# Attention over listed neighbours and a two-of-eight expert layer: gathered-row buffers placed in stage one, second-layer weights loaded from the last values on

## The chip, the cores and the metric

The kernel runs on one core of a Trainium2 chip. The metric is the device time of one execution in microseconds; the median of several runs is compared. One further execution is recorded by the hardware profiler, and all the times inside the kernel come from that one.

## What is computed

There are N = 4096 nodes with 512 features. The reference normalizes them, attends over the neighbours of each node (adjacency plus the node itself) with 8 heads of 64, adds the result to the input, normalizes again and sends each node through the two best of 8 expert networks:

```python
adj = jnp.maximum(adjacency_matrix, eye)
scores = jnp.einsum('hqk,hmk->hqm', q, k) * kd ** (-0.5)
scores = scores + IDENTITY_BIAS * eye - MASK_VAL * (1.0 - adj)
att = jax.nn.softmax(scores, axis=-1)
x = x + jnp.einsum('hqm,hmk,hko->qo', att, v, Wo)
# then, on the normalized x: logits, top 2 of 8 experts, softmax of the two,
h = gelu(jnp.einsum('nd,edh->neh', xf, W1) + b1)
y = jnp.einsum('neh,ehf->nef', h, W2) + b2          # weighted sum of the chosen two
```

The adjacency is sparse and denser for low-numbered nodes. All data are float32.

## The kernel before

The work has three stages, and the nodes are taken in 32 tiles of 128.

**Stage one (lines 186 to 492)** makes keys, values and queries and lists the neighbours. It is a loop of 65 steps, with 8 steps for each block of four tiles. In steps 0 to 3 of a block `project_kv` (L425) makes one tile of keys and values and SP, the engine that issues most transfers, writes it to `kv_d` in HBM (L436); in steps 4 to 7 `project_q` (L438) makes a quarter of the block's queries, and after step 7 SP writes them to `qT_d` (L486). So the last keys and values are made in step 59 and the last queries in step 63. Between these, the transposed adjacency comes in, one 2 MB tile at a time, into three buffers of a pool `adjT` (L258); VectorE (DVE) reduces each to flags (`neighbours`, L262; the last in step 52), and small matrix products, POOL (`begun`, L319) and DVE turn the flags into two lists of row numbers, `key_of` and `mask_of`.

**Stage two (L656 to L982)** is the attention. For each tile the kernel holds a number of chunks of 128 neighbours (28 for the first tile, 8 for the last; 363 in all) and one item for the tile's own nodes: 395 items. Their steps are:

- `fetch` (L714): POOL issues two indirect transfers (L725), one that gathers 128 rows of keys and values from `kv_d` and one that gathers their rows of the adjacency as masks. For the own item SP loads both (L720, L721). There are ten buffers of each in the pool `kv`, and items are fetched nine ahead (`AHEAD`).
- `turn` (L735): TensorE (PE) transposes the keys and ScalarE (ACT) copies them.
- `scores` (L750): PE multiplies, and ACT takes the exponential.
- `masked` (L771): DVE multiplies by the mask.
- `values` (L777): PE adds to the tile's output `po`, and DVE adds to the running sum `acc`.

When a tile is through, its remaining work is spread over the following items in pieces (`piece`, L802): sum, reciprocal, output projection `py`, and the sum with x into a row buffer (L850), which SP writes to `out` (L851). Tiles are joined into groups (seven of 4, then 2, 1 and 1; `GROUPS`, L665). The jobs of a group (`route`, L858) normalize its rows, compute the logits, rank the experts and give each row two places in a table `xs_d`; POOL then scatters the rows there (`route_4`, L591). The row buffers of all groups share one tag with two buffers (L842), and the first write into one is the copy of the row numbers (L845). The first-layer weights `w1` come in during stage two (L947).

After the last item, `finish_routing` (L603) counts the rows of each expert, writes a table of blocks, and has SP write blank rows behind each expert's rows (L650, eight of them) and into a spare block (L644). The spare block's write has to wait for all the scatters, the other eight don't. The second-layer weights `w2`, 8 loads of 1 MB, are issued by ACT after stage two in the text (L988).

**Stage three (L1113 to L1202)** takes 71 blocks of 128 rows: SP loads a block's rows from `xs_d` (L1131), PE multiplies by the two layers, and POOL scatters and adds the result to `out` (L1181).

What sets the order: stage one and the items of stage two are written out by hand (a manual schedule), outside of which a scheduler merges the instructions. Each engine takes its instructions strictly in order, and waits on semaphores. A tile that is placed where an earlier tile lay waits until everything that used the earlier one has ended, and a transfer issued by SP also waits until the one issued eight before it has landed.

Of the kernel before, what the change touches and what calls it, by code (L numbers as in the profile page):

```python
# [10 lines left out]
F32 = mybir.dt.float32  # L11
BF16 = mybir.dt.bfloat16
I32 = mybir.dt.int32
# [6 lines left out]
P = 128  # L20
# [12 lines left out]
def kernel(  # L33
# [31 lines left out]
    nc = tc.nc  # L65
    N, D = x.shape
    H, KD = Wo.shape[0], Wo.shape[1]
    E, _, HID = W1.shape
    DC = D // P
    HC = HID // P  # L70
    NT = N // P
    TB = 512
    NTB = N // TB
    TPB = TB // P
    NP = H * KD // P
    KV = 2 * H * KD
# [5 lines left out]
    W = D + 4  # L82
# [62 lines left out]
    first = const.tile([P, NB], F32, name="first")  # L145
    table = const.tile([1, 2 * NB + E], I32, name="table")
    redo = const.tile([1, 1], I32, name="redo")

    def mean_var(pool, mv, xin, name):

# [27 lines left out]
        nc.scalar.copy(dst, pt)  # L178


    C = N // P
    G = 4
    NX = C + 3
    CHUNK = 14

    with tc.tile_pool(name="adjT", bufs=3) as ap, tc.tile_pool(
        name="wqkv", bufs=1
    ) as wp, tc.tile_pool(name="p1", bufs=3) as work, tc.tile_pool(
        name="p1b", bufs=2
    ) as block, tc.tile_pool(name="lists", bufs=2) as lp, tc.tile_pool(  # L190
        name="ps1t", bufs=2, space=PSUM
# [6 lines left out]

        xts = {}

        def load_x(i):
            xts[i] = work.tile([P, D], F32, tag="xt", bufs=6, name=f"xt_{i}")
            nc.sync.dma_start(out=xts[i], in_=x[ts(i, P), :])

        for i in range(TPB):
            load_x(i)
        for n, src, queue in (("k", Wks, nc.scalar), ("v", Wvs, nc.scalar), ("q", Wqs, nc.sync)):
            for c in range(DC):
                queue.dma_start(out=w[n][:, c], in_=src[ts(c, P), :])
# [243 lines left out]
            tokens_2(t)  # L453
            tokens_3(t)
        for t in range(TPB):
            load_x(TPB + t)
        list_constants()


        load_at = {13 * i // 8: i for i in range(NT)}  # L460
        lists_from = {13 * (g * G + G - 1) // 8 + 3: g for g in range(NTB)}
        for u in range(8 * NTB + 1):
            b, s = divmod(u, 8)
            if u in load_at:
                load_adj(load_at[u])
            due = []
            for k in range(8):
                if u - k in lists_from:
                    due += lists_at(lists_from[u - k], k)
            nxt = (b + 1) * TPB  # L470
            if b < NTB:
                if b + 1 < NTB:
                    if s < 4:
                        tokens_1(nxt + s)
                    else:
                        tokens_2(nxt + s - 4)
                        if b + 2 < NTB:
                            load_x(nxt + TPB + s - 4)
                if s < 4:
                    project_kv(b, s)  # L480
                else:
                    if s == 4:
                        qT = block.tile([P, NP, TB], F32, tag="qT", name=f"qT_{b}")
                    project_q(b, s - 4, qT)
                    if s == 7:
                        nc.sync.dma_start(out=qT_d[:, :, ts(b, TB)], in_=qT)  # L486
                if b + 1 < NTB and s >= 4:
                    tokens_3(nxt + s - 4)
            if u - 2 in load_at:
                neighbours(load_at[u - 2])  # L490
            for f in due:
                f()

# [109 lines left out]
    def finish_routing(pool, psum, blank):  # L603
# [41 lines left out]
        for e in range(E):  # L645
# [5 lines left out]
            for t in scatters:  # L651
# [4 lines left out]
    w1_cm = tc.tile_pool(name="w1", bufs=1)  # L656
    w1p = w1_cm.__enter__()
    w1 = w1p.tile([P, E, DC, HID], F32, name="w1")
    blank = w1p.tile([P, W], F32, name="blank")
    nc.vector.memset(blank, 0.0)  # L660
    nc.gpsimd.iota(blank[:, D : D + 1].bitcast(I32), pattern=[[0, 1]], base=N,
                   channel_multiplier=1)
    nc.sync.dma_start(out=out[N : N + P, :], in_=blank[:, :D])
    AHEAD = 9
    GROUPS = [4] * (NT // 4 - 1) + [2, 1, 1]  # L665
    with tc.tile_pool(name="kv", bufs=AHEAD + 1) as kvp, tc.tile_pool(
        name="p2", bufs=4
    ) as work, tc.tile_pool(name="p2a", bufs=2) as two, tc.tile_pool(
        name="p2o", bufs=1
    ) as single, tc.tile_pool(name="p3", bufs=2) as small, tc.tile_pool(  # L670
        name="ps_s", bufs=3, space=PSUM
    ) as ps_s, tc.tile_pool(name="ps_o", bufs=1, space=PSUM) as ps_o, tc.tile_pool(
        name="ps_k", bufs=1, space=PSUM
    ) as ps_k, tc.tile_pool(name="ps_e", bufs=2, space=PSUM) as ps_e:
        order = tc.manual_schedule()
        order.__enter__()
        ones32 = single.tile([P, Q4], F32, name="ones32")
# [11 lines left out]
        for p in range(NP):  # L689
            u, j = divmod(p, 2)  # L690
            for r in range(2):
# [2 lines left out]
                    spread[:, p, r * KD : (r + 1) * KD],  # L694
                    ident[:, row : row + 1].to_broadcast([P, KD]),
                )
        q_in, x_in, kv, mask, kT, es, po, acc = {}, {}, {}, {}, {}, {}, {}, {}
        items = [(i, c) for i in range(NT) for c in range(-1, listed[i])]
        group_of, groups = {}, []
        for m in GROUPS:  # L700
            i0 = sum(GROUPS[: len(groups)])
# [1 line left out]
            for i in range(i0, i0 + m):  # L703
                group_of[i] = len(groups) - 1

        def load_q(i):
            q_in[i] = two.tile([P, NP, P], F32, tag="q", name=f"q_{i}")
            nc.sync.dma_start(out=q_in[i], in_=qT_d[:, :, ts(i, P)])

        def load_x(i):  # L710
            x_in[i] = two.tile([P, D], F32, tag="xt", name=f"xr_{i}")
            nc.sync.dma_start(out=x_in[i], in_=x[ts(i, P), :])

        def fetch(n):  # L714

            i, c = items[n]
            kv[n] = kvp.tile([P, KV], F32, tag="kv", name=f"kv_{i}_{c}")
            mask[n] = kvp.tile([P, P], F32, tag="mask", name=f"mask_{i}_{c}")
            if c < 0:
                nc.sync.dma_start(out=kv[n], in_=kv_d[ts(i, P), :])  # L720
                nc.sync.dma_start(out=mask[n], in_=adjT[i, ts(i, P), :])  # L721
                return
            s = slice(at[i] + c, at[i] + c + 1)
            for to, src, of in ((kv[n], kv_d, key_of), (mask[n], adjT_rows, mask_of)):
                nc.gpsimd.indirect_dma_start(  # L725
                    out=to, out_offset=None, in_=src,
                    in_offset=bass.IndirectOffsetOnAxis(ap=of[:, s], axis=0),
                )

            if waiting and n % 3 == 0:  # L730
                waiting.pop(0)[1]()

        waiting = []

        def turn(n):  # L735
            kT[n] = work.tile([P, NP, P], F32, tag="kT", bufs=3, name=f"kT_{n}")
# [65 lines left out]
        def piece(i, k):  # L802
# [14 lines left out]
            if k == 2:  # L817
                rinv[i] = single.tile([P, P], F32, tag="rinv", name=f"rinv_{i}")
                nc.vector.reciprocal(rinv[i], sums[i])
                test = single.tile([P, P], F32, tag="test", name=f"test_{i}")  # L820
                nc.scalar.activation(test, sums.pop(i), AF.Copy, accum_out=fine[:, i, 0:1])
                load_x(i)
            if k == 3:
                rb[i] = ps_e.tile([P, NP, P], F32, tag="e", name=f"rb_{i}")
                for p in range(NP):
# [12 lines left out]
            if k == 6:  # L838
                if j == 0:
                    while waiting and waiting[0][0] < g - 1:  # L840
                        waiting.pop(0)[1](True)
                    row[g] = small.tile([P, m, W], F32, tag="rows", name=f"rows_{g}")  # L842
                    lg[g] = small.tile([P, m, E], F32, tag="l", name=f"l_{g}")
                    mv[g] = small.tile([P, m, 4], F32, tag="mv", name=f"mv_{g}")
                    nc.vector.tensor_copy(  # L845
                        row[g][:, :, D].bitcast(I32), ids[:, i0 : i0 + m]
                    )

                y = row[g][:, j, :D] if m > 1 else x_in[i]
                nc.vector.tensor_add(y, x_in[i], py.pop(i))  # L850
                nc.sync.dma_start(out=out[ts(i, P), :], in_=y)  # L851
                mean_var(small, mv[g][:, j], y, f"b{i}")
                if j == m - 1:
                    jobs.extend(route(g))
                if m > 1:
                    x_in.pop(i)
# [70 lines left out]
                if then:  # L927
                    first_of_step.append(then)

        load_q(0)  # L930
        for n in range(AHEAD):
            fetch(n)
        for n in range(3):
            turn(n)
        for n in range(2):
# [3 lines left out]
        for n, (i, c) in enumerate(items):  # L939
            begin()  # L940
            if n + AHEAD < len(items):
                fetch(n + AHEAD)
            if c == 2 and i + 1 < NT:
                load_q(i + 1)
            if n >= 56 and n % 7 == 0 and loads:
                e, d = loads.pop(0)
                nc.sync.dma_start(out=w1[:, e, d], in_=W1[e, ts(d, P), :])  # L947
            if c < 0 and i:
                osb[i - 1] = single.tile([P, NP, P], F32, tag="o", bufs=2, name=f"o_{i - 1}")
                nc.scalar.copy(osb[i - 1], po.pop(i - 1))  # L950
            if n + 3 < len(items):
                turn(n + 3)
            if n + 2 < len(items):
                scores(n + 2)
            values(n)
            later(n)
            if n + 2 < len(items):
                masked(n + 2)
            if c == listed[i] - 1:
                left.append((n, i))  # L960
        order.__exit__(None, None, None)
        osb[NT - 1] = single.tile([P, NP, P], F32, tag="o", bufs=2, name=f"o_{NT - 1}")
        nc.scalar.copy(osb[NT - 1], po.pop(NT - 1))
        n = len(items)
        while n <= len(items) + LAST or jobs or first_of_step:
            begin()
# [14 lines left out]
        nc.tensor.matmul(pf[:1], least, ones32[:, :1], start=True, stop=True)  # L981
        nc.vector.tensor_copy(redo, pf[:1])  # L982

    w2_cm = tc.tile_pool(name="w2", bufs=1)
    w2p = w2_cm.__enter__()
    w2 = w2p.tile([P, E, HC, D], F32, name="w2")
    for e in range(E):
        nc.scalar.dma_start(out=w2[:, e], in_=W2[e].rearrange("(c p) f -> p c f", p=P))  # L988
    with tc.tile_pool(name="end", bufs=1) as pool, tc.tile_pool(
        name="ps_end", bufs=1, space=PSUM  # L990
    ) as psum:
# [254 lines left out]
```

## Time and profile before

| | us |
|---|---|
| median of three runs | 2305.06 |
| lowest and highest run | 2304.19, 2316.68 |
| profiled execution, its span | 2313.0 |
| PE, DVE, ACT, POOL busy | 2114.2, 1534.8, 966.5, 1235.4 |
| stage one, first gather of stage two, first row load of stage three | 0 to 409.3, 415.21, 1745.06 |
| gathers on POOL, 363 of each kind: keys and values, masks | 467.3, 444.5 |

The busy times are sums over three stages that have different limits, so the joins between the stages can't be seen in them. A matrix product's end is modelled in the trace, so a busy PE is not necessarily a PE at its peak. In the lines below, a row of the timeline has its start, its duration, the engine, the line of the kernel, the operation, what it writes and reads, how many such instructions are merged in the row, and in brackets the idle time of that engine ahead of it with what ended it. SPq, ACTq and POOLq are the engines' own queues; a transfer's row on SPq is its issue alone and not the transfer. In the page's groups, the first number after the bar is the busy time in all, the second the mean of one in ns, and after the second bar stand the idle time ahead of them and its releaser.

### The profile page before, as it was taken

To read this page: it belongs to the slowest core of one execution; us is meant where nothing else is said; L and a number is where in the kernel's file an instruction comes from. 1 tells how busy PE (TensorE), PEld (TensorE's weight loads), DVE (VectorE), ACT (ScalarE), POOL (GpSimd) and SP (SyncE) were. 2 spreads that over 40 slices of the span, in tenths; PEclk is the share of its full clock that TensorE was granted. 3 is DMA by queue.
4 is the path that set the end of the run, shared out by engine and by line. 5 is a ranking of instruction groups with operands and counts; after the bars stand their busy time and mean duration, and the time that the engine had idled before them with its cause. 6 is when DMAs were issued, how large, how long until landed. Compare 5 with 4: busy or idle time off the path is not lost. (4 is left out here: it accounts for less than half of the span.)

```text
span 2313.0 us, 51031 instructions
## 1 busy us (share of the span) xinstructions
PE 2114.2 (91%) x20304; PEld 1419.3 (61%) x20304; DVE 1534.8 (66%) x2300; ACT 966.5 (42%) x1834; POOL 1235.4 (53%) x943
## 2 busy tenths in 40 slices
PE   7789999789999989989999999999837999999998
PEld 3344444577777777777777777777623444444444
DVE  4889983588888878878878879788752232323232
ACT  2122222455556556556556565556411222222221
POOL 1434331678887787787787878778511121221212
PEclk9899999899999999999999999999958999999999
DMA  7767881677777777767677776767565655565554
GB/s 295 289 240 290 312 309 64 196 217 215 227 223 235 238 223 240 233 221 248 211 232 237 234 236 213 229 210 233 171 214 143 135 133 137 135 143 131 136 138 91
DMA packets 176722, 477.36 MB, mean 206 GB/s; under 512 B 23089, under 2 KB 43569, under 8 KB 172386
## 3 DMA queue, kind: packets, MB, share of 16 engines
q0 software_dynamic: 79232, 249.68, 36.9%
q1 hardware_dynamic: 91874, 213.87, 28.3%
q10 hardware_dynamic: 5376, 10.49, 1.4%
q8 instruction: 165, 2.70, 0.5%
q14 instruction: 75, 0.61, 0.1%
HBM read 402.23 MB, written 71.72 MB: 205 GB/s over the span
## 5 line engine op out<-in xcount | busy, mean ns | idle before, releaser
L775 DVE TENSOR_TENSOR e<-e,mask 128x1024 f32<-128x1024 f32 x363 | 443.8, 1223 | 163.7 <-ACT e L768 161.3
L725 POOL DMA_INDIRECT kv<-kv_d,key_of x363 | 467.3, 1287 | 129.1 <-issue 48.8
L725 POOL DMA_INDIRECT mask<-in_adjT_dram,mask_of x363 | 444.5, 1225 | 111.6 <-issue 80.8
L793 DVE TENSOR_TENSOR acc<-acc,e 128x1024 f32<-128x1024 f32 x363 | 442.6, 1219 | 0.0
L768 ACT ACTIVATE e<-s 128x512 f32<-128x512 f32 x726 | 394.5, 596 | 105.3 <-PE s L758 102.3
L758 PE MATMUL s<-q,kT 64*128 64x128 f32 x5808 | 420.4, 285 | 0.3 <-ACT acc L768 0.3
L787 PE MATMUL po<-e,kv 128*64 128x128 f32 x5808 | 408.1, 284 | 2.8 <-DVE e L775 2.8
L745 ACT COPY kT<-pk 128x512 f32<-128x512 f32 x395 | 231.6, 586 | 347.4 <-PE pk L742 343.7
L758 PEld LDWEIGHTS s<-q,kT 64*128 64x128 f32 x5808 | 371.6, 194 | 0.6 <-ACT acc L768 0.6
L1181 POOL DMA_INDIRECT out_dram<-y,r x71 | 110.8, 1560 | 467.5 <-ACT y L1180 298.4
L787 PEld LDWEIGHTS po<-e,kv 128*64 128x64 f32 x5808 | 318.9, 140 | 48.2 <-DVE e L775 3.2
L324 POOL TENSOR_SCALAR started<-slots,base 128x1152 bf16<-128x1152 f32 (+11 forms) x32 | 126.0, 3941 | 251.2 <-DVE longer L295 156.2
L1145 PE MATMUL ph<-w,xT 128*128 x568 | 258.7, 598 | 1.0 <-ACT xT L178 1.0
L1174 PE MATMUL py<-w,hT 128*128 x568 | 255.6, 593 | 0.9 <-DVE hT L1159 0.9
L742 PE MATMUL pk<-ident,kv 64*128 64x64 f32 x2904 | 171.4, 238 | 76.0 <-DMA kv<-kv_d,key_of 62.0
L742 PEld LDWEIGHTS pk<-ident,kv 64*128 64x128 f32 x2904 | 123.1, 141 | 155.4 <-issue 98.8
L1179 DVE TENSOR_TENSOR y<-py,bb 128x512 f32<-128x512 f32 x71 | 49.1, 691 | 225.6 <-PE py L1174 209.7
L1145 PEld LDWEIGHTS ph<-w,xT 128*128 128x128 f32 x568 | 103.5, 193 | 104.6 <-issue 103.0
L1174 PEld LDWEIGHTS py<-w,hT 128*128 128x128 f32 x568 | 102.7, 191 | 103.9 <-issue 102.7
L267 DVE TENSOR_REDUCE flags<-adjT 128x32 f32<-128x4096 f32 x32 | 140.7, 4402 | 21.6 <-DMA adjT<-in_adjT_dram 21.6
L1150 DVE TENSOR_TENSOR h<-ph,bb 128x512 f32<-128x512 f32 x71 | 49.1, 691 | 141.5 <-PE ph L1145 141.5
L1180 ACT ACTIVATE y<-y,gate 128x512 f32<-128x512 f32 x71 | 51.2, 721 | 213.1 <-DVE y L1179 213.1
(576 smaller groups left out, 2251.0 us busy)
## 6 DMA issues: line engine op xcount, KB each, us to landing
adjT<-in_adjT_dram SPq DMA_DIRECT2D x32, 2048.0 KB
bb<-in_L_ffn_b_dram SPq DMA_DIRECT2D x142, 256.0 KB
r<-xs_d SPq DMA_DIRECT2D x71, 258.0 KB
kv_d<-kv SPq DMA_DIRECT2D x32, 512.0 KB
xt<-in_x_dram SPq DMA_DIRECT2D x32, 256.0 KB
qT_d<-qT SPq DMA_DIRECT2D x8, 1024.0 KB
q<-qT_d SPq DMA_DIRECT2D x32, 256.0 KB
xr<-in_x_dram SPq DMA_DIRECT2D x32, 256.0 KB
```

The costliest lines, as they stand in the source:

```text
L267: nc.vector.tensor_reduce(flags[g][:, j, :], adj_in.pop(i), axis=AX.X, op=ALU.max)
L324: nc.gpsimd.tensor_scalar(started[i], slots[:, :n], base[g][:, j : j + 1], None, op0=ALU.is_ge)
L725: nc.gpsimd.indirect_dma_start(out=to, out_offset=None, in_=src, in_offset=bass.IndirectOffsetOnAxis(ap=of[:, s], axis=0),)
L742: nc.tensor.transpose(pk[:, r, ts(p, KD)], kv[n][half, ts(p, P)], ident[half, half])
L745: nc.scalar.copy(kT[n].rearrange("k p (r j) -> k r p j", r=2), pk[:, :, : NP * KD].rearrange("k r (p j) -> k r p j", p=NP),)
L758: nc.tensor.matmul(s[r][:, p, :], k[rows, p, :], q_in[i][rows, p, :], start=True, stop=True,)
L768: nc.scalar.activation(e[:, r * NP : (r + 1) * NP], s[r], AF.Exp)
L775: nc.vector.tensor_mul(e, e, m.unsqueeze(1).to_broadcast([P, 2 * NP, P]))
L787: nc.tensor.matmul(po[i][r * KD : (r + 1) * KD, p, :], v[:, ts(h, KD)], e[:, r * NP + p, :], start=(c < 0 and p == 0), stop=(c == listed[i ...
L793: nc.vector.tensor_add(acc[i], acc[i], e)
L1145: nc.tensor.matmul(ph, xTs[b][:, c, :], w1[:, bass.ds(es[b], 1), c, :], start=(c == 0), stop=(c == DC - 1),)
L1174: nc.tensor.matmul(py, hTs[b][:, c, :], w2[:, bass.ds(es[b], 1), c, :], start=(c == 0), stop=(c == HC - 1),)
```

## The change

1. The pool `adjT` is opened on the right-hand side of the on-chip memory, and closed in stage one as soon as the last adjacency tile has been reduced (step 52). The pools for gathered rows (`kv`) and queries (`q`) are opened in its place there; the first query tile and the first own item are loaded then, and items 1 to 8 are fetched in step 60. Before, all of them were issued at the start of stage two.
2. The blank tile is made among the constants, and its write to `out` is issued at the start of stage one instead of between the stages.
3. A tile's x rows are loaded at its third item instead of after its last.
4. Row buffers have a tag for each group size: groups of four share two buffers, the group of two has one, and the groups of one have two.
5. After the last item the pools `p2`, `q` and `kv` are closed, and `w2` takes their place. SP issues its eight loads, inside the manual schedule, ahead of the last tile's remaining pieces; before, ACT issued them.

```diff
+    blank = const.tile([P, W], F32, name="blank")
+    nc.vector.memset(blank, 0.0)
+    nc.gpsimd.iota(blank[:, D : D + 1].bitcast(I32), pattern=[[0, 1]], base=N,
+                   channel_multiplier=1)
...
-    with tc.tile_pool(name="adjT", bufs=3) as ap, tc.tile_pool(
+    ap_cm = tc.tile_pool(name="adjT", bufs=3, side="right")
+    ap = ap_cm.__enter__()
...
         list_constants()
+        nc.sync.dma_start(out=out[N : N + P, :], in_=blank[:, :D])
...
                 neighbours(load_at[u - 2])
+                if load_at[u - 2] == NT - 1:
+                    ap_cm.__exit__(None, None, None)
+                    kv_cm = tc.tile_pool(name="kv", bufs=AHEAD + 1, side="right")
+                    kvp = kv_cm.__enter__()
+                    q_cm = tc.tile_pool(name="q", bufs=2, side="right")
+                    qp = q_cm.__enter__()
+                    load_q(0)
+                    fetch(0)
+            if u == 8 * NTB - 4:
+                for n in range(1, AHEAD):
+                    fetch(n)
...
-    nc.sync.dma_start(out=out[N : N + P, :], in_=blank[:, :D])
...
-                load_x(i)
...
-                    row[g] = small.tile([P, m, W], F32, tag="rows", name=f"rows_{g}")
+                    row[g] = small.tile(
+                        [P, m, W], F32, tag=f"rows{m}", bufs=1 if m == 2 else 2, name=f"rows_{g}"
+                    )
...
-        load_q(0)
-        for n in range(AHEAD):
-            fetch(n)
...
                 load_q(i + 1)
+            if c == 2:
+                load_x(i)
...
-        order.__exit__(None, None, None)
         osb[NT - 1] = single.tile([P, NP, P], F32, tag="o", bufs=2, name=f"o_{NT - 1}")
         nc.scalar.copy(osb[NT - 1], po.pop(NT - 1))
+        work_cm.__exit__(None, None, None)
+        q_cm.__exit__(None, None, None)
+        kv_cm.__exit__(None, None, None)
+        w2_cm = tc.tile_pool(name="w2", bufs=1, side="right")
+        w2p = w2_cm.__enter__()
+        w2 = w2p.tile([P, E, HC, D], F32, name="w2")
+        for e in range(E):
+            nc.sync.dma_start(out=w2[:, e], in_=W2[e].rearrange("(c p) f -> p c f", p=P))
+        order.__exit__(None, None, None)
...
-    for e in range(E):
-        nc.scalar.dma_start(out=w2[:, e], in_=W2[e].rearrange("(c p) f -> p c f", p=P))
```

More of the change, by code (lines that the diff above doesn't have):

```diff
@@ L178, in transposed, with load_q, fetch @@
         nc.scalar.copy(dst, pt)
+    AHEAD = 9
+    items = [(i, c) for i in range(NT) for c in range(-1, listed[i])]
+    q_in, kv, mask = {}, {}, {}
+    waiting = []
+    def load_q(i):
+        q_in[i] = qp.tile([P, NP, P], F32, tag="q", name=f"q_{i}")
+        nc.sync.dma_start(out=q_in[i], in_=qT_d[:, :, ts(i, P)])
+    def fetch(n):
+        i, c = items[n]
+        kv[n] = kvp.tile([P, KV], F32, tag="kv", name=f"kv_{i}_{c}")
+        mask[n] = kvp.tile([P, P], F32, tag="mask", name=f"mask_{i}_{c}")
+        if c < 0:
+            nc.sync.dma_start(out=kv[n], in_=kv_d[ts(i, P), :])
+            nc.sync.dma_start(out=mask[n], in_=adjT[i, ts(i, P), :])
+            return
+        s = slice(at[i] + c, at[i] + c + 1)
+        for to, src, of in ((kv[n], kv_d, key_of), (mask[n], adjT_rows, mask_of)):
+            nc.gpsimd.indirect_dma_start(
+                out=to, out_offset=None, in_=src,
+                in_offset=bass.IndirectOffsetOnAxis(ap=of[:, s], axis=0),
+            )
+        if waiting and n % 3 == 0:
+            waiting.pop(0)[1]()
     C = N // P
@@ L184 @@
     CHUNK = 14
-    with tc.tile_pool(name="adjT", bufs=3) as ap, tc.tile_pool(
-        name="wqkv", bufs=1
-    ) as wp, tc.tile_pool(name="p1", bufs=3) as work, tc.tile_pool(
+    ap_cm = tc.tile_pool(name="adjT", bufs=3, side="right")
+    ap = ap_cm.__enter__()
+    with tc.tile_pool(name="wqkv", bufs=1) as wp, tc.tile_pool(name="p1", bufs=3) as work, tc.tile_pool(
         name="p1b", bufs=2
@@ L199, with load_x1 @@
         xts = {}
-        def load_x(i):
+        def load_x1(i):
             xts[i] = work.tile([P, D], F32, tag="xt", bufs=6, name=f"xt_{i}")
@@ L205 @@
         for i in range(TPB):
-            load_x(i)
+            load_x1(i)
         for n, src, queue in (("k", Wks, nc.scalar), ("v", Wvs, nc.scalar), ("q", Wqs, nc.sync)):
@@ L455 @@
         for t in range(TPB):
-            load_x(TPB + t)
+            load_x1(TPB + t)
         list_constants()
+        nc.sync.dma_start(out=out[N : N + P, :], in_=blank[:, :D])
         load_at = {13 * i // 8: i for i in range(NT)}
@@ L477 @@
                         if b + 2 < NTB:
-                            load_x(nxt + TPB + s - 4)
+                            load_x1(nxt + TPB + s - 4)
                 if s < 4:
@@ L658 @@
     w1 = w1p.tile([P, E, DC, HID], F32, name="w1")
[L659 to L662, printed above, removed]
-    nc.sync.dma_start(out=out[N : N + P, :], in_=blank[:, :D])
-    AHEAD = 9
     GROUPS = [4] * (NT // 4 - 1) + [2, 1, 1]
-    with tc.tile_pool(name="kv", bufs=AHEAD + 1) as kvp, tc.tile_pool(
-        name="p2", bufs=4
-    ) as work, tc.tile_pool(name="p2a", bufs=2) as two, tc.tile_pool(
+    with tc.tile_pool(name="p2a", bufs=2) as two, tc.tile_pool(
         name="p2o", bufs=1
@@ L674 @@
     ) as ps_k, tc.tile_pool(name="ps_e", bufs=2, space=PSUM) as ps_e:
+        work_cm = tc.tile_pool(name="p2", bufs=4)
+        work = work_cm.__enter__()
         order = tc.manual_schedule()
@@ L696 @@
                 )
-        q_in, x_in, kv, mask, kT, es, po, acc = {}, {}, {}, {}, {}, {}, {}, {}
-        items = [(i, c) for i in range(NT) for c in range(-1, listed[i])]
+        x_in, kT, es, po, acc = {}, {}, {}, {}, {}
         group_of, groups = {}, []
@@ L704 @@
                 group_of[i] = len(groups) - 1
-        def load_q(i):
-            q_in[i] = two.tile([P, NP, P], F32, tag="q", name=f"q_{i}")
-            nc.sync.dma_start(out=q_in[i], in_=qT_d[:, :, ts(i, P)])
         def load_x(i):
@@ L712, in load_x @@
             nc.sync.dma_start(out=x_in[i], in_=x[ts(i, P), :])
[L714 to L733, printed above, removed]
         def turn(n):
@@ L821, in piece @@
                 nc.scalar.activation(test, sums.pop(i), AF.Copy, accum_out=fine[:, i, 0:1])
-                load_x(i)
             if k == 3:
@@ L841, in piece @@
                         waiting.pop(0)[1](True)
-                    row[g] = small.tile([P, m, W], F32, tag="rows", name=f"rows_{g}")
+                    row[g] = small.tile(
+                        [P, m, W], F32, tag=f"rows{m}", bufs=1 if m == 2 else 2, name=f"rows_{g}"
+                    )
                     lg[g] = small.tile([P, m, E], F32, tag="l", name=f"l_{g}")
@@ L982 @@
         nc.vector.tensor_copy(redo, pf[:1])
-    w2_cm = tc.tile_pool(name="w2", bufs=1)
-    w2p = w2_cm.__enter__()
-    w2 = w2p.tile([P, E, HC, D], F32, name="w2")
-    for e in range(E):
-        nc.scalar.dma_start(out=w2[:, e], in_=W2[e].rearrange("(c p) f -> p c f", p=P))
     with tc.tile_pool(name="end", bufs=1) as pool, tc.tile_pool(
```

## The prediction

> **What bounds the kernel now.** The page was read first, then the windows view with one row for each stage, then the timeline across the two joins between stages, and last the instruction order of the two built programs with the semaphores each instruction waits for (that order holds no times). The page names the gathers:
>
> ```profile
> L725 POOL DMA_INDIRECT kv<-kv_d,key_of x363 | 467.3, 1287 | 129.1 <-issue 48.8
> L725 POOL DMA_INDIRECT mask<-in_adjT_dram,mask_of x363 | 444.5, 1225 | 111.6 <-issue 80.8
> ```
>
> The windows view (columns: window; its length, then busy us and count of PE, PEld, DVE, ACT, POOL; granted TensorE clock, DMA share, GB/s) gives projection, the first join, attention, the second join and the experts:
>
> ```profile
> 350.00:409.30 59.30, 59.28 (x197) 27.38 (x195) 18.08 (x69) 14.37 (x25) 11.37 (x4) 1.00 0.16 62
> 409.30:433.00 23.70, 9.91 (x106) 9.01 (x106) 3.72 (x5) 6.09 (x11) 13.95 (x15) 0.64 0.74 253
> 433.00:1640.00 1207.00, 1129.33 (x16694) 925.52 (x16690) 1003.10 (x1168) 706.42 (x1388) 955.56 (x756) 0.98 0.73 227
> 1640.00:1745.00 105.00, 51.95 (x529) 37.88 (x525) 55.41 (x184) 24.09 (x54) 22.81 (x21) 0.68 0.50 172
> 1745.00:2313.00 568.00, 554.27 (x1704) 272.93 (x1704) 167.89 (x355) 131.85 (x214) 110.79 (x71) 0.99 0.58 132
> ```
>
> Stages one and three are TensorE's. In stage two the bound is POOL: 955.56 us busy, and the timeline shows a gap of 0.30 us, rarely more, ahead of each of its 756 DMA instructions, 227 us; together 1182 of 1207 us. POOL works through its list from the first gather to the last with hardly a pause, so the stage starts when the first gather does. The two joins (23.7 and 105 us) are where PE stands still. The first, in the timeline:
>
> ```profile
> 395.90 0.33 SPq L436 DMA_DIRECT2D kv_d<-kv  x1
> ...
> 409.94 0.55 SPq L486 DMA_DIRECT2D qT_d<-qT  x1
> 415.21 1.19 POOL L725 DMA_INDIRECT kv<-kv_d,key_of  x1 [5.06 <-DMA out_dram<-blank]
> 419.69 0.69 PE L742 MATMUL pk<-ident,kv_-1_2607 64*128 64x64 f32 x8 [10.41 <-issue]
> ...
> 431.65 1.09 PE L787 MATMUL po<-acc,kv_-1_2607 128*64 128x128 f32 x16
> ```
>
> The last keys and values are written at 395.90, yet the first gather starts at 415.21: by the built order it waits for the last q write too (L486, issued 409.94), because its buffer lies where stage one's tiles were. The second join:
>
> ```profile
> 1680.04 0.15 DVE L845 CAST rows<-ids 128x1 int32<-128x1 f32 x1 [7.43 <-DMA xs_d<-rows,slot_i]
> ...
> 1690.29 0.58 ACT L963 COPY o<-po 128x512 f32<-128x512 f32 x1 [1.57 <-PE po L787]
> ...
> 1715.59 0.15 DVE L845 CAST rows<-ids 128x1 int32<-128x1 f32 x1 [9.35 <-DMA xs_d<-rows,slot_i]
> ...
> 1736.16 0.34 SPq L644 DMA_DIRECT2D xs_d<-blank  x1
> 1737.00 3.01 SPq L650 DMA_DIRECT2D xs_d<-blank  x4
> ...
> 1745.06 0.38 SPq L1131 DMA_DIRECT2D r<-xs_d  x1
> ```
>
> Twice VectorE, with the last masks and the routing queued behind, waits for scatters that still read a row buffer: two buffers serve all groups.
>
> **What the Trainium skill says.** (1) "DMA: Bandwidth & Descriptors", section "Queues, rings and completion order": SP and ACT each own one ring on each of the same 16 DMA engines, and an engine takes a ring's descriptors in order. So loads moved from ACT to SP stand ahead of everything SP issues later; the trace of before shows them as a queue of their own (q10, 10.49 MB) and no such case. (2) The same page, "Issuing engines are not separate DMA queues": the move saves only issue time; the trace has 0.37 us for each. (3) The same page, "Anatomy of one DMA — SWDGE (gpsimd) path": about 2.0 us fixed. The trace agrees where nothing else moves: a scatter's landing frees the next one 2.04 us after its issue ends. (4) "TensorE: Matmul & The Clock Gate", "Part 1: The HAM clock gate": half clock after an idle window of some 3.4 us. The trace shows it after less: four transposes take 1.09 us instead of 0.66 behind a gap of 2.43 us.
>
> **The change, part by part.** The order of PE's instructions does not change at all; of the times below, those of the second join are on the old timeline, as if stage two had started as before.
>
> *Gathers in stage one.* In the built order the first gather now waits for nothing later than the last kv_d write. That write is issued at 395.90 and the DMA view shows its traffic ending at 398.25; before, traffic ended at about 414.5 and the gather started 0.7 us later. So the first gather goes to 398.9 instead of 415.21: **16.3 us**. POOL has no other work there (its last list task ends at 384.15). What could eat it: the first exponential on ACT and the first constants on DVE (1.8 us of them, previously at 397.4, hidden) now wait for the q write, since their tiles lie over it. It is issued at 409.94; 1 MB took 3.5 us alone, and beside the gathers at half of the 400 GB/s seen I take 5.5, so 416.5. Constants 1.8, mask 0.3 and 1.2 and the values' 1.1 bring item 0 to 421; POOL needs that buffer again for its tenth pair, at 398.9 + 9 x 2.49 = 421.3 (a pair is 0.94 + 0.95 + 2 x 0.30 here). It just fits. A cold TensorE (item 0's scores 1.86 to 2.1 instead of 1.11) may delay the next buffers: 0 to 3 us, 1.0 taken. **Gain 15.3 (13.3 to 16.3)**, kept to the end because POOL bounds the stage.
>
> *Own row buffers by group size* (tags rows4, rows2, rows1). The CAST at 1680.04 and the one at 1715.59 wait for no scatter. Without the first, VectorE adds py when PE ends it, 1673.95 instead of 1680.14; 3.48 us of statistics as before put the next mask at 1677.4 and the last, 2.6 later, at 1680.0; the last values end near 1683.1 and o is copied at 1683.2 instead of 1690.29: 7.1. The output projection ran at half clock, 6.41 us against 3.70 elsewhere; whether PE stays warm is open (0 to 4 us; 1.3 taken): tile 31's sum at 1693.8 instead of 1702.23, 8.4. Without the second wait the last two groups' routing and statistics interleave (some 6 us, from their rows), so the last normalization moves from 1718.14 to 1699.8: 18.3. From there the same chain, with the table's operations now behind the last scatter's (1.1 us): last scatter at 1709.8 instead of 1729.20. The waits don't vanish: the slot tile, also double, waits for the same scatters, but later, when they have landed (1680, and about 1702 to 1708).
>
> *The blank writes.* Before, four of the eight per-expert blanks went out ahead of the one that waits for all scatters (1736.16) and four behind; now all eight stand behind it: four more at 0.93 us, **3.7 lost**. The last scatter landed 6.0 us after its issue ended, beside 1 MB of those blanks; now 2.0 to 6.0, 3.0 taken: landing 1713.7. Then 0.84, 7 x 0.93 and the 5.4 from last blank to first row: row load at 1726.4 instead of 1745.06, **18.7 (13 to 23)**.
>
> *Second-layer weights on SP.* Their buffer is free when the last value product and sum are done, 1684. Eight loads, 8.39 MB at the 345 to 406 GB/s seen for them, are in by about 1706; beside 1 MB of scatters, 1708. Behind them in SP's queue stand tile 31's output row (the table waits for its landing: about 1709, against 1708 from its own chain) and the blanks (1713.7). Nothing waits longer: **0 (0 to −3, contained above)**. ACT loses eight issues of 0.37 us, beside PE work: 0.
>
> *The rest at 0:* the blank tile's memset (0.49), iota (0.13) and 256 KB write move to the start, where DVE waits 3.23 us for x and PE for weights; the x rows load one tile earlier, never waited for before or after; the q and blank writes leave the first join, counted above. The write delays stage one's first adjacency load by up to 0.8 us, on no path to PE.
>
> **Sum:** 15.3 + 18.7 = 34.0. The profiled span of 2313.0 becomes 2279.0; that execution stands near the top of the three runs (2304.19 to 2316.68). The terms are waits of fixed length, so I take them from the median: 2305.06 − 34.0 = **2271.1**.
>
> **Rivals.** *Only the start gains.* Another wait takes the place of the row buffers (PE cold throughout, scatters slowed by 8 MB beside them): the tail keeps 5 of 18.7, so 2305.1 − 20.3 = 2284.8. For it: the half clock from 1680 to 1702. Against: both CASTs are released by scatters by name. *Only the tail gains.* The early gathers fill ten buffers and stand still until the q write lets item 0 through; were that 10 us later than I hold, 5 of the 15.3 stay: 2305.1 − 5 − 18.7 = 2281.4. Against: 9 pairs take 22 us to issue. *No change to speak of:* both halves fail, 2300. *Slower: the weights block SP.* With blanks and output rows behind them on one ring, the row load comes 7.3 us after the last weight lands (two more blanks at 0.93, then 5.4). It cancels the whole gain if the weights finish at 1753 instead of 1706, that is below 8.39 MB / 69 us = 122 GB/s; at 100 they end at 1768 and the time is 2305.1 + 15 = 2320. The trace has no such rate for them.
>
> **How the numbers follow.** Both gains 0.62 (2264 to 2279 from the bounds: 34.0 − 7.7 to 34.0 + 5.3, rounded out by the spread of runs), start only 0.15, tail only 0.10, no change 0.08, slower 0.05. A measurement of this kernel can tell about 0.5% (11.5 us) from no change: faster 0.87, same 0.08, slower 0.05. The range 2262 to 2286 takes in the first three cases.
>
> **What would show it.** First gather near 399 and still 0.30 us between POOL's instructions; first values near 420; no DVE wait on scatters at the last two CASTs; weights landed before the first blank; row load some 34 us earlier. I am wrong if POOL pauses for buffers early in stage two, if the table waits for the output row behind the weights, or if stage two's pace of 3.1 us a pair changes.

## The result, and the profile after

| | before | after |
|---|---|---|
| median of four runs of each, us | 2305.03 | 2277.14 |
| lowest and highest | 2304.19, 2316.68 | 2275.15, 2280.64 |
| profiled execution, its span | 2313.0 | 2273.4 |

The changed kernel takes 0.987 of the time before (95% interval 0.9841 to 0.9899), 27.9 us less where 34.0 were forecast. The forecast of 2271.1 is 6 us too low and its range holds the time. The two profiled executions differ by 39.6 us, because that of before was a long one and that of the changed kernel the shortest of its four.

In the changed kernel the lines have other numbers: gathers L205, CAST L860, residual add L865, scatters L638, blanks L690 and L696, row load L1149. Its windows view, cut at the same joins (window; its length; busy us and count of PE, PEld, DVE, ACT, POOL; TensorE's granted clock; DMA share; GB/s):

```profile
409.30:433.00 23.70, 19.82 (x242) 16.45 (x242) 12.27 (x24) 11.54 (x21) 18.82 (x17) 0.78 0.84 268
433.00:1620.00 1187.00, 1114.32 (x16580) 911.69 (x16579) 996.78 (x1164) 702.08 (x1381) 943.28 (x748) 0.99 0.73 229
1620.00:1706.00 86.00, 45.34 (x509) 32.68 (x505) 53.39 (x181) 23.45 (x52) 23.20 (x22) 0.75 0.57 205
1706.00:2273.00 567.00, 552.76 (x1704) 272.41 (x1704) 167.63 (x355) 131.80 (x214) 110.79 (x71) 0.99 0.59 132
```

In the first row PE now works twice as long (19.82 us instead of 9.91, of which some 2 us are the end of stage one, which came later); the second join lasts 86 us instead of 105; attention and the experts look as before. The first join, in the timeline of the changed kernel:

```profile
398.10 0.33 SPq L469 DMA_DIRECT2D kv_d<-kv  x1
402.22 1.18 POOL L205 DMA_INDIRECT kv<-kv_d,key_of  x1 [15.87 <-issue]
403.70 0.96 POOL L205 DMA_INDIRECT mask<-in_adjT_dram,mask_of  x1 [0.30 <-issue]
...
412.13 0.59 SPq L520 DMA_DIRECT2D qT_d<-qT  x1
...
418.59 0.09 DVE L718 MEMSET ones<- 128x32 f32 x1 [18.83 <-DMA qT_d<-qT]
...
423.55 1.44 PE L801 MATMUL po<-acc,kv_-1_2301 128*64 128x128 f32 x16
```

The first gather starts at 402.22 instead of 415.21 and no longer waits for the q write, which is issued ten us later. In the trace of before, the bracket at the first gather names the write of the blank rows, which SP issued at 410.60, just behind the q write. It was moved too, and no run moves it alone; but its 256 KB take only some 0.65 us at the 401 GB/s that the transfers moved then (an estimate from these figures), so nearly all of that wait goes back to the q write. DVE's first constants wait for that write now. Item 0's values start at 423.55 instead of 431.65, and POOL's pauses up to 450 are still 0.30 us each. The last kv_d write stands at 398.10, though, and before at 395.90. The second join:

```profile
1649.99 0.21 DVE L860 CAST rows<-ids 128x1 int32<-128x1 f32 x2
1651.26 0.69 DVE L865 TENSOR_TENSOR xr<-xr,py 128x512 f32<-128x512 f32 x1 [1.06 <-PE py L848]
...
1661.11 16.36 SPq L985 DMA_DIRECT2D w<-in_L_ffn_W_dram  x8
...
1677.58 2.90 SPq L866 DMA_DIRECT2D out_dram<-xr  x1
...
1686.87 0.97 POOL L638 DMA_INDIRECT xs_d<-rows,slot_i  x1 [0.30 <-issue]
1691.94 0.17 DVE L654 COPY many<-pn 128x8 f32<-128x8 f32 x1 [7.13 <-DMA out_dram<-xr]
1692.75 0.36 SPq L690 DMA_DIRECT2D xs_d<-blank  x1
1694.30 6.86 SPq L696 DMA_DIRECT2D xs_d<-blank  x8
1706.32 0.38 SPq L1149 DMA_DIRECT2D r<-xs_d  x1
```

The two CASTs stand in one row and wait for nothing. In their place there is one new wait, 7.13 us ahead of the counts (`many`), for tile 31's output row: SP issued it at 1677.58, behind eight weight loads whose issue alone took 16.36 us. From the end of the last gather (1646.41 before, 1626.64 here) to the first row load of stage three, which I call the tail from here on, before took 98.65 us and this kernel 79.68.

### The profile page after: what moved, and what is told of

The parts are those of the page before. It is cut to its first block, busy times and chain, and to the rows that moved or that the text cites. A ratio compares the mean times of both kernels' runs of the same rounds, so it can differ in the third digit from the quotient of the medians.

```text
span 2273.4 us, 51021 instructions
## 1 busy us (share of the span) xinstructions
PE 2101.1 (92%) x20304; PEld 1407.2 (62%) x20304; DVE 1533.7 (67%) x2300; ACT 966.7 (43%) x1834; POOL 1234.1 (54%) x943
## 5 line engine op out<-in xcount | busy, mean ns | idle before, releaser
L205 POOL DMA_INDIRECT kv<-kv_d,key_of x363 | 451.1, 1243 | 137.7 <-issue 63.1
L205 POOL DMA_INDIRECT mask<-in_adjT_dram,mask_of x363 | 458.7, 1264 | 110.7 <-issue 79.9
L772 PE MATMUL s<-q,kT 64*128 64x128 f32 x5808 | 414.9, 282 | 1.7 <-ACT acc L782 1.7
L801 PE MATMUL po<-e,kv 128*64 128x128 f32 x5808 | 402.0, 281 | 0.0
L772 PEld LDWEIGHTS s<-q,kT 64*128 64x128 f32 x5808 | 366.6, 192 | 2.0 <-ACT acc L782 2.0
L801 PEld LDWEIGHTS po<-e,kv 128*64 128x64 f32 x5808 | 313.6, 138 | 44.4 <-issue 1.5
```

What stands on the lines that cost most here:

```text
L205: nc.gpsimd.indirect_dma_start(out=to, out_offset=None, in_=src, in_offset=bass.IndirectOffsetOnAxis(ap=of[:, s], axis=0),)
L772: nc.tensor.matmul(s[r][:, p, :], k[rows, p, :], q_in[i][rows, p, :], start=True, stop=True,)
L801: nc.tensor.matmul(po[i][r * KD : (r + 1) * KD, p, :], v[:, ts(h, KD)], e[:, r * NP + p, :], start=(c < 0 and p == 0), stop=(c == listed[i ...
```

## The experiments

Twelve runs were made, of eleven kernels. Their totals vary by about as much as the smaller parts are worth, so each is also read by stages of its trace. The first four ran on a chip whose granted clock in stage two was lower (0.91 to 0.92 against 0.98 to 0.99; the kernel before took 2500.87 us there); it is called the first chip below. There POOL waited for PE in stage two, as its largest group in the lines view of "row buffers alone" tells, where the values (`po`) end most of its idle time:

```profile
L725 POOL DMA_INDIRECT kv<-kv_d,key_of x363 | 473.6, 1305 | 320.9 <-PE po L787 179.8 <-issue 46.0 <-PE pk L742 40.0
```

So their totals aren't set beside those of the other chips, and of their stages only those outside of stage two are used. All times are us; the ratio is to the kernel before on the same chip, with its 95% interval.

| kernel | first gather | stage two | tail | stage three | ratio |
|---|---|---|---|---|---|
| before, two traces | 415.21, 415.03 | 1231.2, 1227.5 | 98.65, 96.07 | 567.9, 568.1 | |
| after, two traces | 402.22, 402.33 | 1224.4, 1234.7 | 79.68, 80.66 | 567.1, 567.5 | 0.9881 (0.9833 to 0.993), second time |
| row buffers alone (first chip) | 414.35 | – | 77.72 | 570.3 | 0.993 (0.991 to 0.9949) |
| row buffers alone, again | 417.31 | 1225.3 | 79.25 | 568.8 | 0.9939 (0.9921 to 0.9957) |
| weights on SP alone | 416.31 | 1226.7 | 89.27 | 568.2 | 0.9972 (0.9957 to 0.9987) |
| gathers alone | 400.88 | 1223.9 | 97.20 | 571.6 | 0.994 (0.9924 to 0.9955) |
| after with one row tag (first chip) | 401.13 | – | 88.32 | 567.7 | 0.9923 (0.9888 to 0.9959) |
| after, weights on ACT as before | 402.78 | 1220.6 | 78.82 | 567.2 | 0.9878 (0.9859 to 0.9897) |
| after, weights on SP around the output row | 402.26 | 1229.5 | 82.28 | 572.1 | 0.9871 (0.9846 to 0.9896) |
| after, weights last of all (first chip) | 402.80 | – | 85.14 | 579.2 | 0.9941 (0.992 to 0.9962) |
| gathers alone, weights last (first chip) | 400.14 | – | 93.15 | 578.6 | 0.9976 (0.9955 to 0.9998) |
| after, blank write in stage two | 404.53 | 1232.5 | 82.01 | 567.9 | 0.9898 (0.9846 to 0.9951) |

*The two kernels once more*, for a profile of each from one chip. Each repeats its own stages to within 3 us in the tail and some 10 us in stage two; the first profile of before had a tail 2.6 us longer than the second.

> The kernel before, unchanged, to have its profile from the same chip as the runs sent with it. Both theories: the same stages as in the first profile: first gather at 414 to 416, 97 to 99 us from the end of the last gather to the load of stage three, stage three 567 to 570. The time of stage two may differ with the granted clock.

> The changed kernel, unchanged, as the reference of this chip. First gather at 401 to 403, 79 to 81 us from the last gather to the load of stage three, stage three 567; a gain of 28 to 34 us over the kernel before if stage two takes the same time in both.

Two figures missed what was expected: the tail of before, 96.07, is under 97, and the gain, 27.4 us by the ratio, is under 28, with stage two 7 us longer in the changed kernel's trace than in that of before.

*Row buffers alone.* In the kernel before:

```diff
-                    row[g] = small.tile([P, m, W], F32, tag="rows", name=f"rows_{g}")
+                    row[g] = small.tile(
+                        [P, m, W], F32, tag=f"rows{m}", bufs=1 if m == 2 else 2, name=f"rows_{g}"
+                    )
```

> The kernel before with the row buffers by group size alone. Theory (the tail's gain is that of the row buffers, because the last two groups no longer wait for group 7's buffer): the same 19 us that the two traces showed from the last gather to the load of stage three, so 2305.0 - 19.0 = 2286; the second-layer weights stay at the end, so the last scatter lands in about 2 us instead of 4.9 and the time may be up to 3 us shorter still (2283). Rival (the early weights made the tail shorter, by taking 8 MB away from the start of stage three): 2300 to 2305. In the trace: the CAST into tile 31's rows has no wait, first gather still at 415.

> The kernel before with the row buffers by group size alone, once more, beside the two runs sent with it. Theory: from the last gather to the load of stage three 77 to 79 us instead of 96 to 98.7, so 19 us shorter, ratio 0.9917; together with the gathers' 0.9944 this gives 0.986, so the two parts account for the whole change. Rival (the weights on SP are needed for the whole gain): the two ratios multiply to 0.989 or more.

The tail fell to 77.72 and 79.25 us: the row buffers alone do all that the changed kernel's tail shows, and a little more. The rival that the early weights did it falls. An earlier landing of the last scatter, for which up to 3 us more were expected, did not come: the spare block's blank went out 6.3 and 6.7 us after that scatter's issue had ended. By the ratio the kernel is 17.5 us faster on the first chip and 14 us (10 to 18) in the second run, which is below the 19 expected. In the trace of the second run stage one ended later than in that of the first (first gather 417.31 against 414.35), where nothing was edited; whether that is the reason is not shown.

*The changed kernel with one row tag* undoes that edit.

> The changed kernel with one row buffer tag again, as before. Theory: the wait of the CAST for group 7's scatters comes back, +19 us on 2277.1, so 2296. Rival (the early weights carry the tail's gain): 2277 to 2280. If the two parts need each other, both this run and the one with the row buffers alone miss 19.

My theory failed here. The CAST's waits came back, but the tail was 88.32 us, so undoing the edit costs some 8 us and not 19. In the timelines of DVE, first of the kernel before (second trace), then of this kernel:

```profile
1674.45 0.15 DVE L845 CAST rows<-ids 128x1 int32<-128x1 f32 x1 [7.67 <-DMA xs_d<-rows,slot_i]
...
1696.13 0.69 DVE L850 TENSOR_TENSOR xr<-xr,py 128x512 f32<-128x512 f32 x1 [4.58 <-PE py L835]
1697.46 0.15 DVE L585 TENSOR_TENSOR rows<-more,rows 128x2 f32<-128x2 f32 x1
1709.23 0.15 DVE L845 CAST rows<-ids 128x1 int32<-128x1 f32 x1 [9.09 <-DMA xs_d<-rows,slot_i]
```

```profile
1859.83 0.15 DVE L858 CAST rows<-ids 128x1 int32<-128x1 f32 x1 [7.66 <-DMA xs_d<-rows,slot_i]
...
1876.73 0.16 DVE L631 TENSOR_TENSOR rows<-more,rows 128x2 f32<-128x2 f32 x1
1881.34 0.69 DVE L863 TENSOR_TENSOR xr<-xr,py 128x512 f32<-128x512 f32 x1 [4.44 <-PE py L848]
1888.93 0.15 DVE L858 CAST rows<-ids 128x1 int32<-128x1 f32 x1 [4.14 <-DMA xs_d<-rows,slot_i]
```

The shape 128x2 is the group of two (group 8). Before, its last operation stands behind tile 31's residual add, which waits for tile 31's projection; group 8's four scatters wait for that operation, and the second CAST waits for the scatters. With the weights on SP that operation stands ahead of the add. Nothing in the edit names these instructions. My reading was that the scheduler, which merges the text after the manual part, places them otherwise when ACT's queue has no weight loads to issue.

*The weights on SP alone.* One word in the kernel before was to show that:

```diff
-        nc.scalar.dma_start(out=w2[:, e], in_=W2[e].rearrange("(c p) f -> p c f", p=P))
+        nc.sync.dma_start(out=w2[:, e], in_=W2[e].rearrange("(c p) f -> p c f", p=P))
```

> The kernel before with one word changed: the second-layer weights issued on SP instead of ScalarE; pools, row tags and gathers as before. Theory (the scheduler, freed of eight issues on ScalarE's queue, places group 8's last two operations on VectorE ahead of tile 31's residual add, so its four scatters no longer wait for tile 31's projection, and the second wait of the CAST is shorter): group 8's scatters 7 to 9 us earlier counted from the last gather, the second CAST wait 4 us instead of 9.4, the load of stage three 88 to 91 us after the last gather instead of 97 to 99. Rival (where the weights are issued costs nothing, as the prediction has it): 97 to 99 us stays.

It did. The timeline of DVE:

```profile
1692.22 0.16 DVE L585 TENSOR_TENSOR rows<-more,rows 128x2 f32<-128x2 f32 x1
1696.93 0.69 DVE L850 TENSOR_TENSOR xr<-xr,py 128x512 f32<-128x512 f32 x1 [4.54 <-PE py L835]
1700.84 0.15 DVE L845 CAST rows<-ids 128x1 int32<-128x1 f32 x1 [0.45 <-DMA xs_d<-rows,slot_i]
```

Group 8's operation precedes the add, the second wait is 0.45 us instead of 9.09, the tail is 89.27 us and the kernel 6.5 us faster by its ratio. Group 8's first scatter came 5.7 us earlier after the last gather (50.1 against 55.8), less than the 7 to 9 expected.

*The weights in the changed kernel.* If the row buffers leave nothing that waits for group 8's scatters, SP is no longer worth anything there. Three placements were tried. In the first the weights come last of all, in a pool opened after the attention's pools are closed; the same was done with one row tag.

> The changed kernel with the second-layer weights loaded after the last routing on ScalarE's queue, as before. Theory (the early load is no gain; on SP's ring it stood in front of tile 31's output row and made the last scatter's landing longer): DVE's 7.13 us wait ahead of the counts goes, the last scatter lands in 2 to 3 us instead of 4.9, so 1.5 to 4 us shorter than 2277.1, about 2274.5. Rival (stage three's start needs the weights early): 2282 or more, with the load of stage three's second layer waited for.

> The changed kernel with one row tag and the second-layer weights loaded at the end on ScalarE's queue, so that only the gathers in stage one (with the pools, the blank rows and the x loads that go with them) remain. Theory (POOL's chain of gathers bounds stage two, so it shifts whole with its first gather, 13.0 us earlier): 2305.0 - 13.0 = 2292. Rival (part of the shift is lost on the way, because medians differ by 27.9 and not by 13.0 + 19.0): 27.9 - 19.0 = 8.9 earlier, 2296.

```diff
-        w2_cm = tc.tile_pool(name="w2", bufs=1, side="right")
...
-            nc.sync.dma_start(out=w2[:, e], in_=W2[e].rearrange("(c p) f -> p c f", p=P))
...
+    w2_cm = tc.tile_pool(name="w2", bufs=1)
...
+        nc.scalar.dma_start(out=w2[:, e], in_=W2[e].rearrange("(c p) f -> p c f", p=P))
     with tc.tile_pool(name="end", bufs=1) as pool, tc.tile_pool(
```

These two don't put back the state before, as their expectations assume: the kernel before issues the loads on ACT spread over the tail (1684.92 to 1715.30 in its second trace), and here all eight come at the end of it, with 33.5 and 34 us of issue. In both, group 8's operation stands ahead of the add, so that order goes with the loads that are missing on ACT there, and not with loads on SP. Stage three grew by 11 us (579.2, 578.6), so the rival is right that late weights cost, but not by the way it named: the second layer's first products start without a wait. The first layer's do wait. They start 17.6 us after the first row load instead of 5.2 in the changed kernel (weights last of all, timelines of ACT and PE):

```profile
1881.40 33.48 ACTq L1006 DMA_DIRECT2D w<-in_L_ffn_W_dram  x8
1915.31 1.07 ACT L182 COPY xT<-pt_e 128x512 f32<-128x512 f32 x2 [43.41 <-DMA bb<-in_L_ffn_b_dram]
...
1915.94 8.60 PE L1163 MATMUL ph<-w,xT 128*128 x16 [4.77 <-ACT xT L182]
```

They need ACT's copy of the transposed rows, and that copy stands in ACT's queue behind the eight loads, whose issue ends at 1914.88. PE began to transpose the first rows at 1905.69, 7.3 us after the row load where the changed kernel takes 3.35: so some 4 us of the 12.4 are rows and biases that came later beside the 8 MB, and the rest is ACT. The end of the tail is longer beside the 8 MB too: from the spare block's blank to the first row load it takes 17.6 us in both kernels, 8.9 in the kernel before and 13.6 in the changed one. So neither theory can be read from the totals: the changed kernel was not run on that chip, and the 6 us (0.5 to 11) that the gathers alone gain there by the ratio have the longer stage three in them.

In the other two placements the pool stays where the change opens it, and the loads stand ahead of the last checks of the tail, where the scheduler spreads them; in this form on ACT, in the other on SP:

```diff
-        for e in range(E):
-            nc.sync.dma_start(out=w2[:, e], in_=W2[e].rearrange("(c p) f -> p c f", p=P))
         order.__exit__(None, None, None)
...
+        for e in range(E):
+            nc.scalar.dma_start(out=w2[:, e], in_=W2[e].rearrange("(c p) f -> p c f", p=P))
         bad = small.tile([P, NT, 3], F32, name="bad")
```

> The changed kernel with the second-layer weights on ScalarE's queue again, in the order in which the kernel before issues them; gathers in stage one and row buffers by group size stay. Theory (with the row buffers apart, the place of the weights decides nothing, because nothing waits for group 8's scatters any more; on SP they only stand in front of tile 31's output row): from the last gather to the load of stage three 77 to 78.5 us instead of 79.7 to 80.7, DVE's wait for the output row of tile 31 gone, so 2 us shorter than the changed kernel, ratio to before about 0.987. Rival (the 6.8 us that the weights on SP saved in the kernel before are part of the changed kernel's gain): 86 to 87 us, 2284.

> The changed kernel with the weights issued on SP where the scheduler places them: three loads ahead of tile 31's output row and five behind it, instead of all eight ahead. Theory: the output row lands earlier, DVE's wait for it falls from 7 us to under 3, and the load of stage three comes 0.5 to 1.5 us earlier counted from the last gather than in the changed kernel (78 to 79.5). Rival (the last scatter's landing under the weights' traffic decides): 80 or more, with the last scatter landing 5 us or more after its issue.

On ACT, SP's timeline at the end of the tail reads:

```profile
1683.29 3.14 SPq L696 DMA_DIRECT2D xs_d<-blank  x4
1693.20 0.34 SPq L690 DMA_DIRECT2D xs_d<-blank  x1
1694.04 2.97 SPq L696 DMA_DIRECT2D xs_d<-blank  x4
1702.21 0.38 SPq L1149 DMA_DIRECT2D r<-xs_d  x1
```

Four blanks go out ahead of the one that waits for the scatters, as before, DVE's wait for the output row is gone, and the tail is 78.82 us, 1 to 3 less than in the traces of the changed kernel. The rival's 86 to 87 did not come: the 7 to 8 us that SP saves alone are no part of the gain. The form on SP, with three loads ahead of the output row and five behind, was no better than the change (82.28, and 572.1 in stage three). Its theory failed: DVE's wait for the output row was gone there too, but the tail got no shorter. The spare block's blank went out 5.4 us after the last scatter's issue had ended, as its rival said, and all eight other blanks stand behind it.

*Gathers alone*: the form with the weights on ACT, with one row tag.

> The changed kernel with one row tag and the weights on ScalarE's queue in the order of the kernel before: the gathers in stage one alone. Theory: first gather at 400 to 404.5 instead of 415, 96 to 98.7 us from the last gather to the load of stage three as in the kernel before, stage two as long as before to within its spread (1224 to 1235 on the chips seen first), so 13 us shorter, ratio 0.9944. Rival (the earlier start is partly lost in stage two): ratio 0.997 or more, stage two longer by some 5 us.

It held: first gather 400.88, stage two 1223.9, tail 97.20, and 13.8 us faster by its ratio. This kernel also has the earlier blank write and x loads of the change (parts 2 and 3); no run gives the x loads apart.

*The blank write.* In both traces of the changed kernel the last kv_d write is some 2.2 to 2.5 us later than before. In the timeline of PE (changed kernel):

```profile
65.18 0.17 PE L320 MATMUL pb<-x,below 128*128 128x4 bf16 x1 [1.55 <-DVE x L314]
...
75.22 0.22 PE L347 MATMUL pd<-x,step 128*128 128x140 bf16 x1 [2.87 <-DVE stats_a L156]
75.28 5.34 PE L464 MATMUL pk<-wk,xT 128*128 128x512 f32 x8
```

The same eight products took 3.65 us before, with pauses of 0.83 and 2.87 us ahead. I took the blank write for the cause of the longer first pause:

```diff
-        nc.sync.dma_start(out=out[N : N + P, :], in_=blank[:, :D])
...
+            if n == 40:
+                nc.sync.dma_start(out=out[N : N + P, :], in_=blank[:, :D])
```

> The changed kernel with the write of the blank rows to the output moved from the start of stage one into stage two (beside gather 40). Theory (the 256 KB lie in front of an adjacency load at the start, VectorE gets it 0.7 us later, TensorE's pause grows from 0.8 to 1.55 us and its clock then drops to half for some 1.7 us more): last kv_d write of stage one and the first gather 2.2 us earlier than in the changed kernel, first gather at 400. Rival (the 2.2 us come from something else in stage one, the pools on the other side or the memory layout): first gather stays at 402.2. Everything after the first gather as in the changed kernel, so about 2275 where that takes 2277.

That fell as well. The first gather came at 404.53, later than with the write in its place, and the products took 6.66 us. Two kernels with the blank write at the start had their first gather at 400.14 and 400.88, and the kernel with the row buffers alone, run on two chips, ended stage one 3 us apart. Nor does the length of the first pause decide: with the weights on ACT it was 0.87 us and the products took 5.12, where before 0.83 us went with 3.65. So nothing here puts the 2.2 us down to the blank write. What decides whether PE's clock falls there stays open.

## Why the prediction was right, and where it was not

**The bound.** Stage two starts with its first gather and shifts whole. Off the first chip it took 1225.3 to 1231.2 us in the four traces without early gathers and 1220.6 to 1234.7 in the six with them; both means are 1228. Within that spread nothing of the earlier start is lost there, and the kernel with the gathers alone gains 13.8 us (10 to 18) in its total, so the rival "only the tail gains" is out; POOL does not stand still for the q write, as the prediction held.

**Gathers, 15.3.** The path was right and the size a little off, inside the range given. The means over all traces are 415.6 without and 402.1 with early gathers: 13.5. The term that was too large is the 16.3 to the first gather: it needs 4.1 us after the issue of the last kv_d write (402.22 − 398.10, and 400.88 − 396.77), where 3.0 were taken; the rest is stage one's varying end. Whether the 1.0 set aside for a cold TensorE was needed can't be told from the spread of stage two.

**Row buffers and the tail, 18.7.** The row buffers alone make the tail 78.6 (three traces with the weights on ACT) instead of 97.3 (three with one tag and the weights on ACT), 18.7. The changed kernel has 80.8 (its two traces and that of the blank write), 16.5. So the sum of the tail was right for the first profiled pair (98.65 − 79.68 = 19.0) and 2 us high on the mean. That the row buffers alone also give 18.7 is chance: the forecast's sum holds 3.0 for an earlier landing of the last scatter, which that kernel doesn't show, and takes off 3.7 for blanks, which it doesn't lose. Errors of both signs met in the sum. In the first pair, counted from the last gather, o was copied 10.2 us earlier (7.1 forecast), although the py product still ran at half clock (6.11 us). In the means of the changed kernel's three traces and of the three with one tag and the weights on ACT, the last scatter was issued 21.2 earlier (19.4 forecast) and landed after 5.5 us instead of 5.9 (3.0 forecast); the first blank behind it lost 1.1, and four more blanks 4.0: 21.2 + 0.4 − 1.1 − 4.0 = 16.5. The landing is the term that was mis-sized most.

**Weights on SP, 0.** This step was wrong in its reason, though the number is near. It took the issuing queue as the only thing that moves. The scheduler orders DVE and SP anew, and the 3.7 us of blanks behind the waiting one, which the prediction booked as a part of its own, are the weights' doing too: they vanish with the weights on ACT. Worth 7 to 8 us alone, the move is worth about −2 together with the row buffers, since both take away the same second wait. The −2 is read from the tails; the totals, 0.987 and 0.9881 against 0.9878, can't tell it. "The table waits for tile 31's output row" was the condition named for being wrong there; it does, for 7.13 us, of which the first blank to follow loses under 1 (1.55 us behind the spare block's blank instead of 0.84 in the first pair).

**The sum.** 13.5 + 16.5 = 30.0 against 27.9 (23 to 37 by the interval). The parts alone also give the whole: 0.994 × 0.9939 = 0.988, against 0.9878 for the two together with the weights on ACT. That lies between the 0.986 and the 0.989 named beforehand for the second run of the row buffers alone, and its interval reaches past both; that the weights on SP are not needed is shown by the kernel that has the rest without them. So neither rival with half a gain holds. "Slower" needed 122 GB/s or less while the weights load; in the second trace of the changed kernel the windows from 1680 to 1690 and 1690 to 1700 us moved 373 and 392 GB/s.

**A better kernel?** The change with the weights back on ACT has the shortest profiled span, 2269.4, and 0.9878 as ratio; that is not to be told from 0.987 and 0.9881. No version here beats the change beyond doubt.

## What to carry to other kernels

A chain of gathers that one engine issues without a pause can be started as soon as its source is written: take from its buffers every tile that makes the first one wait for something later. When two edits take away the same wait, measure each alone and both together, since their gains don't add. And compare the written order of the instructions on every engine after moving a transfer between queues: where a scheduler merges, the move can reorder an engine that the edit doesn't name.

## What the runs showed of the hardware

"TensorE: Matmul & The Clock Gate", "Part 1: The HAM clock gate", of the Trainium skill has the half clock after an idle window of some 3.4 us. Here pauses of 1.55 and 2.87 us, 10 us apart, were followed by eight products at 5.34 us instead of 3.65; pauses of 1.57 and 2.87 us in the kernel with the gathers alone were not (3.65 us), and pauses of 0.87 and 2.87 us with the weights on ACT were (5.12 us). The length of the pauses alone does not decide.

The same kernel took 8% longer on one chip than elsewhere (2500.87 against 2305 to 2307 us), nearly all in stage two: 1423 instead of 1225 us for the kernel with the row buffers alone, at a granted clock of 0.91 instead of 0.98. PE's busy time in that stage was 1272 instead of 1143 us for the same products, which is 129 of the 198 us; why the clock was lower and where the rest comes from is not shown. In stage three that chip granted 0.99 as elsewhere, and stages one and three and the tail differed by a few us at most.
